# A selective-scan layer: a chunk's preparation laid over 19 states instead of 15, and the norm after the scan with its 1/std per token

## The chip, the cores and the metric

The kernel runs on one core of a Trainium2 chip. It computes a four-layer network in one launch; the change lies wholly in the first layer. The metric is the device time of one execution in microseconds (us). In the text PE is TensorE, DVE is VectorE, ACT is ScalarE, POOL is GpSimd and SP is SyncE, which only issues transfers here. Each engine runs its own instructions strictly in the order in which the program lists them, and waits where one of them needs something that another engine has not yet produced.

## The reference

Layer 0 is a two-dimensional selective scan over an image of 64 x 64 tokens, two images in the batch. After an input projection and a depthwise 3 x 3 convolution, the tokens are read in four orders (the four values of `kk`), and for each order a recurrence with 16 states per channel runs along the 4096 tokens of the image:

```python
delta = softplus(delta + delta_bias)
def step(h, inp):
    ut, dt, bt, ct = inp
    dA = exp(dt[..., None] * A4)
    h = dA * h + (dt * ut)[..., None] * bt[:, :, None, :]
    y = einsum('bkdn,bkn->bkd', h, ct)
    return (h, y)
...
y = y + u * D
# sum over the four orders, then
y = layernorm(y, eps=1e-5) * ln_w + ln_b     # over the 256 inner channels
y = y * silu(z)
x = x + y @ W_out.T
```

There are 256 inner channels (two halves of 128 partitions, `h` in the kernel), 16 states, and the result is added to the layer's input. Layers 1 to 3 (a deformable convolution, a state-space layer with a spectral filter, a linear attention and a mixture of experts) follow and are the same in both kernels.

## The kernel before, in words

`layer0` handles the two images one after the other. For each image it has three stages.

**Before the scan** (lines 195 to 236) it normalises, projects and convolves; the branch `z` goes to DRAM as `zs`, and the scan's input `U` stays in SBUF.

**The scan** (lines 238 to 406) goes through 32 chunks of 512 tokens, in the order given by `todo`: eight chunks for each of the four reading orders 0, 2, 1, 3. Inside a chunk there is a loop over the 16 states, `n`. One state is this chain:

- POOL multiplies `du` by one row of B, giving `S` (L365, 128 x 1024), and, except in the first chunk of an order, adds the state carried over from the chunk before (L371, two columns).
- ACT computes `dA = exp(dt * A)` in two halves (L374). There are two `dA` tiles, so ACT can be at most two states ahead of DVE.
- DVE runs the recurrence as one scan instruction over 1024 columns (L376), then multiplies the result by a row of C, `pcn`, giving `M` (L390).
- ACT saves the last column for the next chunk (L378). In the program this save comes one state later, between the next `dA` and that state's share of the preparation.
- PE spreads the row of C over the partitions (L334) and adds `M` up in `yp` through an identity matrix (L405).

`S` has four buffers: the product of state n can be started when `M` of state n-4 is done. B's rows come in groups of four, `br`, through DRAM, by a broadcast transfer that SP issues at n = 2, 6, 10 and 14 (L329). At n = 0 the sums of the chunk before are added to `Y` (`add_up`: on ACT for order 0, L345; on DVE otherwise, L341 and L347), and PE opens the new sums (L387).

Inside this loop the order of instructions is exactly that of the program (`tc.manual_schedule()`); outside it a planner orders them. Between L390 and L334 of each state one step of the generator `prologue` is taken: the preparation of the *next* chunk. Its pieces are separated by `yield`, and `next(steps, None)` takes one piece per state from n = 0; at n = 14 whatever is left is drained. There are 13 pieces, so the last is reached at n = 12:

| n | piece of the preparation |
|---|---|
| 0, 1 | ACT copies `uc`, one half each |
| 2 | PE: projection into PSUM |
| 3 | ACT copies it to `xd` and rounds it to `cs` (bf16); SP writes `bc` to DRAM; PE: first half of `pd` |
| 4, 5 | ACT: absolute value and relu of each half; PE: second half of `pd`; at 5 POOL: remainder `r` (L292) |
| 6 | ACT: two roundings of `r` into `cs` (L296, L297), exponential (L298) |
| 7 | POOL: second remainder (L300); ACT: `u = e + 1` (L301) |
| 8 | POOL: `dt += e` (L303); ACT: rounding (L304), logarithm (L305), with a table load before it and one after it |
| 9 | ACT: `u - 1` (L307) |
| 10, 11, 12 | POOL: `e - u` (L309), `dt += e` (L311), `du = dt * uc` (L313); ACT: `ea` (L318) |

Most tiles of the preparation have two buffers, one for the chunk in use and one for the chunk in preparation.

**The norm and the output projection** (lines 408 to 437) work through the 4096 tokens in eight blocks of 512, with the channels on the partitions: PE takes the mean by a matrix of 1/256 (`pm`), DVE subtracts it (L420), ACT squares (L421), PE averages again (`pq`), `rsqrt` computes 1/std for 128 x 512 values that are equal on all partitions (L81 to L87), DVE applies weight and 1/std (L429), then bias and gate (L430), PE projects to 128 tokens x 128 channels (L434), and DVE adds the result to `X` (L436).

Of the kernel before, what the change touches and what calls it, by code (L numbers as in the profile page):

```python
# [16 lines left out]
F32 = mybir.dt.float32  # L17
I32 = mybir.dt.int32
BF16 = mybir.dt.bfloat16
AF = mybir.ActivationFunctionType  # L20
# [138 lines left out]
def layer0(k):  # L159
# [3 lines left out]
    with ExitStack() as es:  # L163
# [13 lines left out]
            nc.vector.tensor_copy(sel[a : a + 16], k.ident[a : a + 16, a : a + 16].unsqueeze(2).to_broadcast([16, 16, P]))  # L177
        w_out = cst.tile([P, 2, C], F32, name="w_out")
        nc.sync.dma_start(out=w_out, in_=ins["w_out0"].rearrange("(a p) c -> p a c", p=P))
        mean_w = cst.tile([P, P], F32, name="mean_w")  # L180
        nc.vector.memset(mean_w, 1.0 / 256)
        an = cst.tile([P, 8, 16], F32, name="an")
# [9 lines left out]
        for b in range(B):  # L192
# [48 lines left out]
            with ExitStack() as e2:  # L241
# [12 lines left out]
                def prologue(kk, c, got):  # L254


                    uc = ch.tile([P, 2, T], F32, name="uc")
                    for h in range(2):
                        if kk % 2:
                            src = U[:, h, :].rearrange("p (g i w j) -> p w g j i", g=4, i=16, w=4)[:, c // 2, 2 * (c % 2) : 2 * (c % 2) + 2]  # L260
                            for g in range(2):
                                nc.scalar.copy(uc[:, h, g * 256 : (g + 1) * 256].rearrange("p (j i) -> p j i", j=16), src[:, g])
                        else:
                            src = U[:, h, (c // 2) * 1024 : (c // 2 + 1) * 1024].rearrange("p (i w j) -> p w i j", i=16, w=4)
                            for g in range(2):
                                nc.scalar.copy(uc[:, h, g * 256 : (g + 1) * 256].rearrange("p (i j) -> p i j", i=16), src[:, 2 * (c % 2) + g])
                        yield
                    px = ps.tile([P, N], F32, name="pd", tag="ps")
                    for h in range(2):
                        nc.tensor.matmul(px, w_xp[:, h, kk, :], uc[:, h, :], start=h == 0, stop=h == 1)  # L270
                    yield
                    xd = ch.tile([P, T], F32, name="xd")
                    nc.scalar.copy(xd, px)
                    bc = bcp.tile([16, T], F32, name="bc")
                    nc.sync.dma_start(out=bc, in_=xd[112:128, :])

                    cs = ch.tile([80, T], BF16, name="cs")
                    nc.scalar.copy(cs, xd[:80])


                    dt = ch.tile([P, 2, T], F32, name="dt")
                    du = ch.tile([P, 2, T], F32, name="du")
                    e = sm.tile([P, 2, T], F32, name="e")
                    u = sm.tile([P, 2, T], F32, name="u")
                    for h in range(2):
                        bias = k.v("dt_b")[:, kk * 2 + h : kk * 2 + h + 1]
                        pd = ps.tile([P, N], F32, name="pd", tag="ps")
                        nc.tensor.matmul(pd, w_dt[96:104, kk, h * P : (h + 1) * P], xd[96:104, :], start=True, stop=True)
                        yield
                        if h == 1:  # L290
                            r = sm.tile([80, T], F32, name="r")
                            nc.gpsimd.tensor_tensor(r, xd[:80], cs, ALU.subtract)  # L292
                        nc.scalar.activation(e[:, h, :], pd, AF.Abs, bias=bias)
                        nc.scalar.activation(dt[:, h, :], pd, AF.Relu, bias=bias)
                    yield
                    nc.scalar.copy(cs[32:64], r[32:64])  # L296
                    nc.scalar.copy(cs[64:80], r[64:80])  # L297
                    nc.scalar.activation(e, e, AF.Exp, scale=-1.0)  # L298
                    yield
                    nc.gpsimd.tensor_tensor(r[64:80], r[64:80], cs[64:80], ALU.subtract)  # L300
                    nc.scalar.activation(u, e, AF.Identity, bias=1.0)  # L301
                    yield
                    nc.gpsimd.tensor_tensor(dt, dt, e, ALU.add)  # L303
                    nc.scalar.copy(cs[64:80], r[64:80])  # L304
                    nc.scalar.activation(e, u, AF.Ln)  # L305
                    yield
                    nc.scalar.activation(u, u, AF.Identity, bias=-1.0)  # L307
                    yield
                    nc.gpsimd.tensor_tensor(e, e, u, ALU.subtract)  # L309
                    yield  # L310
                    nc.gpsimd.tensor_tensor(dt, dt, e, ALU.add)  # L311
                    yield
                    nc.gpsimd.tensor_tensor(du, dt, uc, ALU.mult)  # L313

                    ea = ch.tile([P, 16, 2], F32, name="ea")
                    f = T - 1 if kk >= 2 else 0
                    for h in range(2):
                        nc.scalar.activation(ea[:, :, h], an[:, kk * 2 + h, :], AF.Exp, scale=dt[:, h, f : f + 1])  # L318
                    got.append((uc, bc, cs, dt, du, ea))
# [7 lines left out]
                def spread(bc, q):  # L327
                    br = wk.tile([P, 4, T], F32, name="br", bufs=2)
                    nc.sync.dma_start(out=br, in_=bc[4 * q : 4 * q + 4, :].partition_broadcast(P))  # L329
                    return br  # L330
# [17 lines left out]

                with tc.manual_schedule():
                    rows, pcn, last, save = spread(ready[0][1], 0), c_row(ready[0][2], 0), None, None  # L350
                    for it, (kk, ci) in enumerate(todo):
                        c = at(it)[1]
                        uc, bc, cs, dt, du, ea = ready.pop()
# [2 lines left out]
                        if ci == 0:  # L356
                            for t in dAs:
                                nc.vector.memset(t[:, :, f : f + 1], 0.0)
                        steps = prologue(*at(it + 1), ready) if it + 1 < len(todo) else iter(())
                        s_ = slice(None, None, -1) if kk >= 2 else slice(None)  # L360
                        for n in range(16):
                            if n % 4 == 0:
# [25 lines left out]
                                last = kk, c, yp  # L388
                            M = wk.tile([P, 2, T], F32, name="M")
                            nc.vector.tensor_tensor(M, S, pcn.unsqueeze(1).to_broadcast([P, 2, T]), ALU.mult)  # L390
                            next(steps, None)
                            if n == 14:
                                for _ in steps:
                                    pass
                            if n < 15:
                                pcn = c_row(cs, n + 1)
# [9 lines left out]
                    add_up(*last)  # L406

            with ExitStack() as e2:
                wk = e2.enter_context(tc.tile_pool(name=f"l0f{b}", bufs=2))
                ps = e2.enter_context(tc.tile_pool(name=f"l0fs{b}", bufs=6, space=PSUM))  # L410
                for q in range(8):
                    s = slice(q * N, (q + 1) * N)
                    zt = wk.tile([P, 2, N], F32, name="zt")
                    nc.sync.dma_start(out=zt, in_=zs[:, :, b * L + q * N : b * L + (q + 1) * N].rearrange("h p t -> p h t"))
                    pm = ps.tile([P, N], F32, name="pm", tag="ps")
                    for h in range(2):
                        nc.tensor.matmul(pm, mean_w, Y[:, h, s], start=h == 0, stop=h == 1)
                    sq = wk.tile([P, 2, N], F32, name="sq")
                    for h in range(2):
                        nc.vector.tensor_tensor(Y[:, h, s], Y[:, h, s], pm, ALU.subtract)  # L420
                        nc.scalar.activation(sq[:, h, :], Y[:, h, s], AF.Square)  # L421
                    pq = ps.tile([P, N], F32, name="pq", tag="ps")
                    for h in range(2):
                        nc.tensor.matmul(pq, mean_w, sq[:, h, :], start=h == 0, stop=h == 1)
                    rs = wk.tile([P, N], F32, name="rs")
                    rsqrt(nc, wk, rs, pq, 1e-5, [P, N], "yn")
                    for h in range(2):
                        o = Y[:, h, s]
                        nc.vector.scalar_tensor_tensor(o, o, k.v("ln_w")[:, h : h + 1], rs, ALU.mult, ALU.mult)  # L429
                        nc.vector.scalar_tensor_tensor(o, o, k.v("ln_b")[:, h : h + 1], zt[:, h, :], ALU.add, ALU.mult)  # L430
                    po = ps.tile([P, N], F32, name="po", tag="ps")
                    for j in range(4):
                        for h in range(2):
                            nc.tensor.matmul(po[:, j * P : (j + 1) * P], Y[:, h, q * N + j * P : q * N + (j + 1) * P], w_out[:, h, :], start=h == 0, stop=h == 1)  # L434
                    o = Xb[:, 4 * q : 4 * q + 4, :]
                    nc.vector.tensor_tensor(o, po.rearrange("p (a c) -> p a c", c=C), o, ALU.add)  # L436
            yb.close()


# [1096 lines left out]
```

## Time and profile before

| | us |
|---|---|
| runs | 15821.19, 15821.78, 15835.69; median 15821.78 |
| the profiled execution | 15825.24 |
| its span in the profile | 15823.2 |
| layer 0, scan of the first image | about 141 to 2104 |
| norm of the first image | 2104 to 2254.6 |
| layer 0, scan of the second image | about 2380 to 4343 |
| norm of the second image | 4343 to 4494 |

The span is the time from the first to the last instruction of the profiled execution; some 2 us lie around it. Layer 0 takes the first 28% of it. Where rows of the profile are shown, a group's row has the line, engine, operation and tile, the number of instructions, their busy time in us and the mean of one in ns, and then the idle time of that engine just before them with what ended it. A row of the timeline has the start in us, the duration in us, and in brackets the idle time before it and its releaser.

### The profile page before, as it was taken

How to read it: one execution, taken by the hardware profiler on the slowest of the kernel's cores; microseconds unless marked ns; L12 is line 12 of the kernel's file. 1: busy time of each engine (PE TensorE's matmuls, PEld its weight loads, DVE VectorE, ACT ScalarE, POOL GpSimd, SP SyncE). 2: the span in 40 equal slices, each digit the busy share in tenths (PEclk: the TensorE clock that was granted, in tenths of full speed). 3: DMA queues.
4: the chain of work that ended last, by engine and by line, in shares of the span. 5: the costliest groups of instructions: out<-in, count | busy, mean ns of one | idle time of the engine just before them, and what ended most of it. 6: DMA issues, size and time to landing. Idle time of an engine off the chain costs nothing.

```text
span 15823.2 us, 190331 instructions
## 1 busy us (share of the span) xinstructions
PE 11939.5 (75%) x69390; PEld 7104.0 (45%) x69390; DVE 13880.2 (88%) x12178; ACT 9839.5 (62%) x15907; POOL 13460.9 (85%) x5140
## 2 busy tenths in 40 slices
PE   6666666666667744567887879879788898898897
PEld 2222222222247721234554546546445555555565
DVE  7999978999954389999999999999999999999974
ACT  5656626666510057777777777777777777777752
POOL 6888828888738889999999999999999999999960
PEclk9999989999978866778998989989999999999998
DMA  2111111111146534455565556556666665665643
GB/s 79 70 70 70 70 44 67 70 70 70 64 143 185 161 133 148 168 172 187 196 193 179 187 179 198 197 185 202 193 190 198 190 204 196 191 203 195 191 163 129
DMA packets 1211433, 2373.40 MB, mean 150 GB/s; under 512 B 346744, under 2 KB 923896, under 8 KB 1044352
## 3 DMA queue, kind: packets, MB, share of 16 engines
q1 hardware_dynamic: 1163072, 2206.74, 42.3%
q0 software_dynamic: 46560, 153.18, 3.2%
q8 instruction: 548, 8.98, 0.2%
q14 instruction: 389, 3.19, 0.1%
q10 hardware_dynamic: 864, 1.32, 0.0%
HBM read 2018.49 MB, written 342.41 MB: 149 GB/s over the span
## 4 chain that ended last, share of the span: by engine, by line
POOL 35%; PE 12%; DVE 11%; DMA 3%; ACT 2%; issue 2%; SPq 0%; POOLq 0%; ACTq 0%; DVEq 0%
POOL S L1110 34%; DVE S L1166 10%; PE pef L994 6%; PE Z L1128 2%; DMA row<-drow 2%; PE acc L967 2%; PE pw L793 1%; POOL S L1116 1%; ACT ze L1134 1%; ACT dA L1164 1%; DMA w<-in_w_b_dram 0%; PE acc L1029 0%; ACT e L974 0%; DMA e<-mdr 0%; PE pt L95 0%
## 5 line engine op out<-in xcount | busy, mean ns | idle before, releaser
L1166 DVE TENSOR_TENSOR_SCAN S<-dA,S 128x512 f32<-128x512 f32 x8192 | 9225.0, 1201 | 385.8 <-ACT dA L1164 207.0
L1110 POOL TENSOR_TENSOR S<-row,g 128x4096 f32<-128x4096 f32 x1024 | 9101.7, 8894 | 266.0 <-DMA row<-drow 224.2
L1164 ACT ACTIVATE dA<-row,a_t 128x512 f32<-128x512 f32 x8192 | 5615.6, 692 | 2141.3 <-DVE S L1166 2108.3
L1128 PE MATMUL Z<-S,cv 128*32 128x256 f32 x32768 | 2506.0, 436 | 1481.7 <-ACT ze L1134 1215.6
L994 PE MATMUL pef<-hk,ur 128*128 128x256 f32 x14336 | 3510.4, 388 | 131.8 <-ACT e L974 120.5
L994 PEld LDWEIGHTS pef<-hk,ur 128*128 128x128 f32 x14336 | 2645.3, 191 | 1070.8 <-issue 562.8
L376 DVE TENSOR_TENSOR_SCAN S<-dA,S 128x1024 f32<-128x1024 f32 x1024 | 2339.1, 2284 | 242.4 <-ACT dA L374 96.1
L365 POOL TENSOR_TENSOR S<-du,br 128x1024 f32<-128x1024 f32 x1024 | 2408.6, 2355 | 137.8 <-DVE M L390 81.0
L1128 PEld LDWEIGHTS Z<-S,cv 128*32 128x32 f32 x32768 | 1002.5, 121 | 2691.5 <-issue 1291.9
L405 PE MATMUL yp<-M,ident 128*128 128x512 f32 x4096 | 2054.6, 626 | 2.9 <-DVE M L390 2.9
L405 PEld LDWEIGHTS yp<-M,ident 128*128 128x128 f32 x4096 | 817.6, 200 | 2092.5 <-issue 2054.1
L374 ACT ACTIVATE dA<-dt,an 128x511 f32<-128x511 f32 x2048 | 1406.9, 687 | 208.1 <-DVE S L376 131.0
L390 DVE TENSOR_TENSOR M<-S,pcn 128x1024 f32<-128x1024 f32 x1024 | 1250.4, 1221 | 106.9 <-DVE S L376 3.7
L334 PE MATMUL pcn<-cs,sel 80*128 80x512 bf16 x1024 | 406.2, 397 | 1188.4 <-DVE M L390 1177.8
L1134 ACT COPY ze<-Z 128x512 f32<-128x512 f32 x1024 | 1123.1, 1097 | 232.4 <-PE Z L1128 200.3
L967 PE MATMUL acc<-e,mw 128*128 128x512 f32 x1920 | 1043.1, 631 | 30.6 <-ACT e L974 29.9
L569 POOL DMA_INDIRECT G<-table,idx x576 | 805.5, 1399 | 203.1 <-issue 170.6
L994 PEld LDWEIGHTS pef<-hd,ur 128*128 128x128 f32 x4096 | 757.8, 194 | 491.1 <-issue 235.2
L994 PE MATMUL pef<-hd,ur 128*128 128x256 f32 (+1 forms) x4096 | 876.4, 340 | 101.5 <-ACT e L974 94.4
L378 ACT COPY stt<-S 128x2 f32<-128x2 f32 x896 | 168.9, 189 | 1082.1 <-DVE S L376 1079.0
L576 DVE TENSOR_TENSOR G<-G,wt 128x4608 f32<-128x4608 f32 x64 | 317.4, 4960 | 572.9 <-DMA G<-table,idx 499.6
L974 ACT COPY e<-pef 128x512 f32<-128x512 f32 x960 | 557.8, 587 | 109.9 <-PE pef L994 61.5
(327 smaller groups left out, 8052.3 us busy)
## 6 DMA issues: line engine op xcount, KB each, us to landing
row<-drow SPq DMA_DIRECT2D x1024, 1024.0 KB
br<-bc SPq DMA_DIRECT2D x256, 1024.0 KB
zd<-ze SPq DMA_DIRECT2D x1024, 256.0 KB
hk<-in_phi_dram SPq DMA_DIRECT2D x128, 576.5 KB
hk<-in_phi_dram SPq DMA_DIRECT2D x96, 704.5 KB
hd<-in_phi_dram SPq DMA_DIRECT2D x512, 128.5 KB
mw<-wdr SPq DMA_DIRECT2D x480, 128.0 KB
hk<-in_phi_dram SPq DMA_DIRECT2D x160, 320.5 KB
```

The costliest lines, as they stand in the source:

```text
L365: nc.gpsimd.tensor_tensor(S, du, br[:, n % 4, :].unsqueeze(1).to_broadcast([P, 2, T]), ALU.mult)
L374: nc.scalar.activation(dA[:, h, rest], dt[:, h, rest], AF.Exp, scale=an[:, kk * 2 + h, n : n + 1])
L376: nc.vector.tensor_tensor_scan(flat, dflat, flat, 0.0, ALU.mult, ALU.add)
L390: nc.vector.tensor_tensor(M, S, pcn.unsqueeze(1).to_broadcast([P, 2, T]), ALU.mult)
L405: nc.tensor.matmul(yp[:, h, :], k.ident, M[:, h, :], start=False, stop=n == 15)
L967: nc.tensor.matmul(acc.rearrange("p a s -> p (a s)"), ms[f][:, o, :], e, start=box["first"], stop="whole" in box and (f, o) == todo[-1])
L994: nc.tensor.matmul(pe[:, a, 256 - n :], ur[:, par, j, :], h[:, at : at + n], start=i == 0, stop=i + 1 == len(mm))
L1110: nc.gpsimd.tensor_tensor(S, row.unsqueeze(1).to_broadcast([P, 2, R, T]), g.unsqueeze(2).to_broadcast([P, 2, R, T]), ALU.mult)
L1128: nc.tensor.matmul(Z[32 * j : 32 * j + 32, q], cv[:, h, s], S[:, h, :, s], start=h == 0, stop=h == 1)
L1134: nc.scalar.copy(ze.rearrange("p q t e -> p q e t"), Z)
L1164: nc.scalar.activation(dA, row[:, j % R, :], AF.Exp, scale=a_t[:, h, d : d + 1])
L1166: nc.vector.tensor_tensor_scan(s, dA, s, 0.0, ALU.mult, ALU.add)
```

## The change

There are two separate parts.

In the scan, three `yield` are added to the preparation: one ahead of the first remainder on POOL (L292), one ahead of the second (L300), and one ahead of `e - u` (L309). That makes 16 pieces. The generator of a chunk is now created two chunks ahead, at n = 12, and waits in the list `soon`; each state takes one piece of every generator in the list. A chunk's preparation so has the states 12 to 15 of one chunk and 0 to 14 of the next, 19 in all, and its last piece is reached at n = 11; the drain at n = 14 stays. The preparation of the very second chunk of an image begins at n = 0, having no earlier chunk to begin in.

In the norm, `mean_w[:, 0:1]` becomes the moving operand and the squares the stationary one, so that the variance comes out with a token per partition: `pv[:, j]`, 128 x 4 values for a block. 1/std is computed on those. Weight and bias of the norm are folded once, at the start, into two copies of the output matrix, `w_ow` and `w_ob`. The gate `z` is applied to the centred `Y` without 1/std; PE then makes two projections, the gated one with `w_ow` and that of the gate with `w_ob`, and DVE multiplies the first by 1/std while it adds both to `X`. The blocks are written so that block q is centred ahead of the projection of block q-1, and the pool has three buffers instead of two.

```diff
+        w_ow = cst.tile([P, 2, C], F32, name="w_ow")
+        w_ob = cst.tile([P, 2, C], F32, name="w_ob")
+        for h in range(2):
+            nc.gpsimd.tensor_scalar(w_ow[:, h, :], w_out[:, h, :], k.v("ln_w")[:, h : h + 1], None, ALU.mult)
+            nc.gpsimd.tensor_scalar(w_ob[:, h, :], w_out[:, h, :], k.v("ln_b")[:, h : h + 1], None, ALU.mult)
...
                         if h == 1:
+                            yield
                             r = sm.tile([80, T], F32, name="r")
                             nc.gpsimd.tensor_tensor(r, xd[:80], cs, ALU.subtract)
...
                     nc.scalar.activation(e, e, AF.Exp, scale=-1.0)
                     yield
+                    yield
                     nc.gpsimd.tensor_tensor(r[64:80], r[64:80], cs[64:80], ALU.subtract)
...
                     nc.scalar.activation(u, u, AF.Identity, bias=-1.0)
+                    yield
                     yield
                     nc.gpsimd.tensor_tensor(e, e, u, ALU.subtract)
...
+                    soon = []
...
-                        steps = prologue(*at(it + 1), ready) if it + 1 < len(todo) else iter(())
+                        if it == 0:
+                            soon.append(prologue(*at(1), ready))
...
-                            next(steps, None)
-                            if n == 14:
-                                for _ in steps:
+                            if n == 12 and it + 2 < len(todo):
+                                soon.append(prologue(*at(it + 2), ready))
+                            for steps in soon:
+                                next(steps, None)
+                            if n == 14 and it + 1 < len(todo):
+                                for _ in soon.pop(0):
                                     pass
...
-                wk = e2.enter_context(tc.tile_pool(name=f"l0f{b}", bufs=2))
+                wk = e2.enter_context(tc.tile_pool(name=f"l0f{b}", bufs=3))
...
+                    nc.scalar.activation(sq, Y[:, :, s], AF.Square)
+                    nc.vector.tensor_tensor(Y[:, :, s], Y[:, :, s], zt, ALU.mult)
+                    return zt, sq
+
+                def projected(q, zt, sq):
+                    pv = ps.tile([P, N], F32, name="pv", tag="ps")
                     for j in range(4):
                         for h in range(2):
+                            nc.tensor.matmul(pv[:, j : j + 1], sq[:, h, j * P : (j + 1) * P], mean_w[:, 0:1], start=h == 0, stop=h == 1)
+                    rs = wk.tile([P, 4], F32, name="rs")
+                    rsqrt(nc, wk, rs, pv[:, :4], 1e-5, [P, 4], "yn")
+                    po = ps.tile([P, 4, C], F32, name="po", tag="ps")
+                    pb = ps.tile([P, 4, C], F32, name="pb", tag="ps")
+                    for o, src, w in ((pb, lambda h, j: zt[:, h, j * P : (j + 1) * P], w_ob), (po, lambda h, j: Y[:, h, q * N + j * P : q * N + (j + 1) * P], w_ow)):
+                        for j in range(4):
+                            for h in range(2):
+                                nc.tensor.matmul(o[:, j, :], src(h, j), w[:, h, :], start=h == 0, stop=h == 1)
                     o = Xb[:, 4 * q : 4 * q + 4, :]
+                    nc.vector.tensor_tensor(o, pb, o, ALU.add)
+                    for j in range(4):
+                        nc.vector.scalar_tensor_tensor(o[:, j, :], po[:, j, :], rs[:, j : j + 1], o[:, j, :], ALU.mult, ALU.add)
+
+                behind = None
+                for q in range(8):
+                    got = centred(q)
+                    if behind is not None:
+                        projected(q - 1, *behind)
+                    behind = got
+                projected(7, *behind)
```

What is left out of the diff in the norm is the old chain: the second average `pq`, `rsqrt` on 128 x 512, L429, L430 and the addition L436.

More of the change, by code (lines that the diff above doesn't have):

```diff
@@ L408, in layer0, with centred @@
             with ExitStack() as e2:
-                wk = e2.enter_context(tc.tile_pool(name=f"l0f{b}", bufs=2))
+                wk = e2.enter_context(tc.tile_pool(name=f"l0f{b}", bufs=3))
                 ps = e2.enter_context(tc.tile_pool(name=f"l0fs{b}", bufs=6, space=PSUM))
-                for q in range(8):
+                def centred(q):
                     s = slice(q * N, (q + 1) * N)
@@ L420, in layer0 @@
                         nc.vector.tensor_tensor(Y[:, h, s], Y[:, h, s], pm, ALU.subtract)
[L421 to L430, printed above, removed]
@@ L431, in layer0 @@
-                    po = ps.tile([P, N], F32, name="po", tag="ps")
+                    nc.scalar.activation(sq, Y[:, :, s], AF.Square)
[3 more added lines that the diff above has]
+                    pv = ps.tile([P, N], F32, name="pv", tag="ps")
                     for j in range(4):
                         for h in range(2):
-                            nc.tensor.matmul(po[:, j * P : (j + 1) * P], Y[:, h, q * N + j * P : q * N + (j + 1) * P], w_out[:, h, :], start=h == 0, stop=h == 1)
@@ L435, in layer0 @@
-                    o = Xb[:, 4 * q : 4 * q + 4, :]
-                    nc.vector.tensor_tensor(o, po.rearrange("p (a c) -> p a c", c=C), o, ALU.add)
+                            nc.tensor.matmul(pv[:, j : j + 1], sq[:, h, j * P : (j + 1) * P], mean_w[:, 0:1], start=h == 0, stop=h == 1)
[3 more added lines that the diff above has]
+                    pb = ps.tile([P, 4, C], F32, name="pb", tag="ps")
```

## The prediction

> **What bounds the kernel now.** I read busy time by stage first: the scan of image 0, then its norm. Columns: stretch, length, then PE, PEld, DVE, ACT and POOL busy, PE's granted clock, DMA share, GB/s.
>
> ```profile
> 141.00:2100.00 1959.00, 1313.40 (x2929) 521.40 (x2929) 1805.45 (x1076) 1186.34 (x2136) 1641.02 (x1203) 0.96 0.19 69
> 2104.00:2180.00 76.00, 31.60 (x97) 18.90 (x97) 44.36 (x51) 8.63 (x13) 0.00 (x0) 0.73 0.09 28
> ```
>
> The scan is DVE's (92%); POOL is close behind (84%). In the norm nobody is busy: DVE has 58%, so a chain across engines is the limit. Next the waits of layer 0, for DVE's scan and for POOL:
>
> ```profile
> POOL r L292 <- ACT cs L278: 364.5, 64, 105.3
> POOL r L300 <- ACT cs L297: 182.5, 64, 3.4
> DVE S L376 <- ACT dA L374: 96.1, 74, 2.4
> DVE S L376 <- POOL S L371: 84.6, 104, 1.8
> POOL e L309 <- ACT u L307: 78.6, 58, 2.8
> DVE S L376 <- POOL S L365: 57.3, 10, 25.5
> ```
>
> DVE loses 242 us ahead of its scans; 51 of the last row are the two images' first states. The timeline of one chunk (state 0 at 692.77, a state every 3.525) shows where the rest sits:
>
> ```profile
> 714.30 1.15 POOL L300 TENSOR_TENSOR r<-r,cs 16x512 f32<-16x512 f32 x1 [2.86 <-ACT cs L297]
> ...
> 725.78 2.29 DVE L376 TENSOR_TENSOR_SCAN S<-dA,S 128x1024 f32<-128x1024 f32 x1 [1.20 <-ACT dA L374]
> ...
> 726.82 2.35 POOL L309 TENSOR_TENSOR e<-e,u 128x1024 f32<-128x1024 f32 x1 [1.19 <-ACT u L307]
> ...
> 736.68 2.29 DVE L376 TENSOR_TENSOR_SCAN S<-dA,S 128x1024 f32<-128x1024 f32 x1 [0.24 <-POOL S L371]
> ...
> 741.57 2.29 DVE L376 TENSOR_TENSOR_SCAN S<-dA,S 128x1024 f32<-128x1024 f32 x1 [1.26 <-POOL S L371]
> ```
>
> These are n = 9, 12 and 13, alike in nearly every chunk: 1.20 at n = 9 (sum 67), 0.24 at n = 12 (12), 1.27 at n = 13 (74). At n = 1 another 27, most of it 1.8 to 2.4 in the chunks behind order 0, where ACT copies `Y`. Now one norm block:
>
> ```profile
> 2123.71 1.28 DVE L420 TENSOR_TENSOR Y<-Y,pm 128x512 f32<-128x512 f32 x2 [0.17 <-PE pm L417]
> ...
> 2128.53 3.35 DVE L83 RECIPROCAL rs<-yn_s 128x512 f32<-128x512 f32 x1 [0.69 <-ACT yn_s L82]
> ...
> 2136.68 0.50 PEld L434 LDWEIGHTS po<-w_out,Y 128*128 128x128 f32 x2 [10.41 <-DVE Y L430]
> ...
> 2142.21 0.69 DVE L436 TENSOR_TENSOR X<-po,X 128x512 f32<-128x512 f32 x1 [4.92 <-PE po L434]
> ```
>
> The next block's L420 is at 2143.25: no overlap, 18.8 per block, 150.9 for eight (2103.7 to 2254.6).
>
> **What the Trainium skill says.** "TensorE: Matmul & The Clock Gate", section "What's actually happening", has PE at half clock after an idle window of about 3.4 us and at full clock after a busy one. The trace agrees in direction: 0.96 in the scan, 0.73 in the norm, in steps of 0.5 and 1.0. "GPSIMD Engine Reference", section 4.1, puts two-input elementwise work on POOL at about twice DVE's time; here 2355 ns (L365) against 1221 (L390, same shape). "ScalarE: Activation LUTs", section "What ACT_TABLE_LOAD costs", states 1283 ns and a drain of 1380; this trace has 1283 and the logarithm 0.02 us after it, so I price the load alone.
>
> **The scan, part by part.** No instruction is added. Set state 0's scan to 0 and take state n's at 3.525n. POOL may start product n when `M` of n-4 ends, at 3.525n - 10.6; product, two-column add and gaps take 2.6 (product starts lie 2.58 to 2.6 apart); so POOL can be 8.0 ahead and regains 0.92 per state. Each extra 2.35 costs 2.3, `r` 1.1.
>
> *Before.* `r` at n = 5 stalls 2.4 for ACT. L300 needs L297, done at 21.4 (n = 6), and starts at 21.5. Then product 8 at 22.7, L303, products 9 and 10, `e - u` at 34.0 after 1.2 of waiting, and product 13 is ready at 48.9 against 47.5 due (with the 1.2 of n = 9). That is the measured 1.27: the chain reproduces it.
>
> *After.* Positions: `r` n = 2, L296 to L298 n = 3, L300 n = 5, L303 and the logarithm n = 6, L307 n = 7, L309 n = 9, L311 n = 10, `du` n = 11. `cs` is rounded at n = 15 of the chunk before, ends at -1.9, so `r` at -0.1 finds it. L297 ends at 10.8; POOL comes at 9.6 and waits 1.2, to 12.0. Product 6 then L303: 17.0; product 7: 19.6; 8: 22.2; 9: 24.8. L307 ends at 27.0 (logarithm and both loads at 20.1 to 24.4, `dA`): wait 2.2; L309 29.4; product 10 32.0; L311 34.3; product 11 36.9; `du` 39.3; product 12 ready at 41.9, due 43.4. DVE is not stopped. **Gone: 12 + 74, and about 4 of n = 9's that were POOL's.**
>
> *What stays.* Logarithm and two loads (0.61 + 1.28 + 1.06 + 1.28) move from n = 8 to n = 6; ACT's room between save and next `dA` is about 3.1. The 1.2 reappears at n = 7, 60 times.
>
> *What is late next.* At n = 0 ACT now has `abs` and `relu` (1.37) where it copied half of `uc` (0.81): behind the `Y` copies of order 0 that is 0.57 x 16 = **+9**. On PE the second `pd` (0.9) now stands at n = 0 between L387 and the row of C for n = 1. In orders 1 and 3 that row ends at 7.04 and `M` reads it at 8.15; 7.9 still fits. At half clock it doesn't: three of the first 24 chunks have it, so **+4** with the second chunk's denser preparation. At n = 15 ACT's `xd` waits for PE's projection (two 512-column products behind four of `yp`); by the same sequence at n = 3 before, the following `dA` ends 0.5 before its scan. The rounding of `cs` also waits there for the last reader of the tile two chunks back, L334 at n = 14, already past. SP's queue: `bc` now stands at n = 15, ahead of the broadcast of n = 2, which is issued at -2.0 instead of about -5 and lands 5 later (711.2 to 716.5 in the trace), at 3.0; POOL wants it at 3.5 or later. Scan: -90 + 13 = **-77**, bounds -35 (half the lateness stays at n = 10 to 12) and -95.
>
> **The norm.** Work of one block after. PE: `pm` 4 x 0.43; `po` and `pb` 32 x 0.112 (pitch in the fast part of 2159.6 to 2160.5); `pv` 16 x 0.108 (pitch of L136's pair, one column): 7.0. At half clock 4 x 0.85 + 32 x 0.213 + 16 x 0.17 = 12.9. DVE: L420 1.37; gating 1.22 (as L390); 1/std on 128 x 4 1.36 (the six at 2266.68 to 2268.05 in the group norm); bias sum 0.69; four multiply-adds 0.25 each, from L429's 0.75 for 512 columns: 5.6. ACT 1.3. Gone from DVE: 3.35, 4 x 0.69, 0.43, 2.8. Since block q+1 is centred first, PE never waits for DVE and is the bound. A PE without pauses should mostly hold full clock; I take 8.6 a block, plus 4 to fill and 1.5 to drain: 74 against 151, **-76 per image, -152**. Bounds: 7.0 gives 62 (-178 in all), 12.9 gives 109 (-84). The four folding instructions on POOL (0.6 each, as L217) lie in the first 118 us, where POOL is busy 10. What follows the norm starts when its memory comes free, so it moves up one to one.
>
> **Sum.** -77 - 152 = -229. The profiled execution's 15825.2 becomes 15596; it lies 3.5 above the median shown, so from the median: **15593**. No change is taken as within 0.2% (32 us).
>
> **Rivals.**
> - *POOL's lateness only moves* to n = 10 to 12: for it, three 2.35 in a row and 1.5 of slack at n = 12; against it, the same chain gave n = 13 before to 0.1. Scan +13, sum -139: 15683.
> - *PE stays at half clock in the norm* (0.73 now): norm -84, sum -161: 15661.
> - *Slower: the chunk boundary.* If PE runs at half clock around n = 14 to 1, `yp` and the projection take 3.4 each, `xd` is ready at 7.6 after `M` of 13, `dA` at 10.3 instead of 7.05: 3.3 x 62. The opening sums, `pd` and row at n = 1 end 2.5 late in 48 chunks. 205 + 120 - 90 + 9 - 152: +92, 15914. It decides from about 4 us per boundary. For it: half-clock stretches at 746 to 753. Against: they follow the stall at n = 13, which goes.
> - *The planner* puts the blocks in sequence again and POOL's lateness moves: at half clock a serial block is about 18.5, so near 15820.
>
> **Chances.** Forecast 0.74 (own range 15555 to 15650), POOL 0.10, half clock 0.09, boundary 0.04, planner 0.03. Range 15555 to 15690, reaching to the first two rivals. Faster 0.93, same 0.03, slower 0.04.
>
> **What would show it.** Right: no idle ahead of the scans at n = 12 and 13, 1.2 at n = 7 left, POOL's wait at L292 gone but for the start, L300's near 1.2; a norm near 75 with PE as its busiest engine and a clock near 0.9. Wrong: DVE waiting for `dA` at n = 0 or for `pcn` at n = 1, POOL for `br`, or a norm over 110.

## The result, and the profile after

The changed kernel runs in 15606.35 us (median of four runs, 15597.23 to 15611.47) against 15828.74 for the kernel before (median of four, with the runs taken on the same chip). The ratio is 0.9859, with a 95% interval of 0.9842 to 0.9876: 222 us less at the medians. The forecast was 15593, or 229 less. The profiled execution took 15611.47, its span is 15609.7.

So the gain was forecast to 7 us. Its two terms were not: the scan gave less than forecast and the norm more. The stage table shows it; the columns are stretch, length, busy PE, PEld, DVE, ACT, POOL, then PE's granted clock, DMA share and GB/s. The first row is the scan of image 0, the second its norm.

```profile
143.00:2076.00 1933.00, 1286.47 (x2933) 510.35 (x2932) 1801.42 (x1078) 1185.40 (x2133) 1639.51 (x1201) 0.97 0.19 70
2076.00:2136.10 60.10, 57.98 (x415) 50.20 (x414) 39.85 (x113) 10.83 (x17) 0.00 (x0) 0.97 0.15 45
```

| us, from the timelines | before | after | change | forecast |
|---|---|---|---|---|
| scan, image 0 and image 1 | 1960.2, 1959.8 | 1933.0, 1935.5 | -51.5 | -77 |
| norm, image 0 and image 1 | 150.9, 151.0 | 60.1, 60.3 | -181.5 | -152 |
| between norm 0 and scan 1 | 128.3 | 127.5 | -0.8 | none |

In the norm PE has 58 of 60 us and its clock is 0.97: it has become the bound, as forecast. In the scan DVE is busy as long as before, and what it waits for has changed. The waits of layer 0, with total, number and longest:

```profile
POOL r L299 <- ACT cs L284: 188.6, 2, 101.4
...
POOL e L318 <- ACT u L315: 138.6, 64, 3.3
...
DVE S L387 <- ACT dA L385: 101.9, 75, 2.3
...
POOL r L308 <- ACT cs L304: 65.1, 58, 1.9
...
DVE M L401 <- PE pcn L343: 51.9, 34, 3.2
...
DVE S L387 <- POOL S L376: 51.7, 2, 26.3
```

POOL's wait for the first rounding is left only in the two preparations ahead of the loop (count 2 instead of 64); for the second it is 65.1 / 58 = 1.1 each (forecast 1.2), for `u` 138.6 / 64 = 2.2 (forecast 2.2). DVE's scan no longer waits for POOL at all, but for the first state of each image: the 86 us at n = 12 and 13 are gone. State by state in the timeline, 63.7 of the 101.9 waiting for `dA` lies at n = 7, 1.19 in each of 54 chunks, where the logarithm's step has moved.

The row that was not expected at this size is the fifth. DVE's second operation, `M`, waits for the row of C, and 50.9 of the 51.9 lies at n = 1 of the chunks in orders 1 and 3. One such chunk (the scan of its state 0 starts at 1643.15), in the timeline:

```profile
1645.42 2.41 DVE L350 TENSOR_TENSOR Y<-yp,Y 128x512 f32<-128x512 f32 x2
...
1647.98 3.54 PE L398 MATMUL yp<-uc,dd 128*128 128x512 f32 x4 [2.60 <-DVE Y L350]
...
1651.45 1.19 PE L294 MATMUL pd<-xd,w_dt 8*128 8x512 f32 x2
1652.57 0.39 PE L343 MATMUL pcn<-cs,sel 80*128 80x512 bf16 x1
...
1653.00 1.22 DVE L401 TENSOR_TENSOR M<-S,pcn 128x1024 f32<-128x1024 f32 x1 [1.84 <-PE pcn L343]
```

While DVE adds the old sums to `Y`, PE pauses 2.60. Then the four products that open the new sums take 3.54, `pd` stands behind them, and the row of C ends 9.8 after the scan of state 0; `M` would have started at 8.15. The same place in the kernel before has the same pause, but the products at full speed:

```profile
1675.62 1.95 PE L387 MATMUL yp<-uc,dd 128*128 128x512 f32 x4 [2.61 <-DVE Y L341]
1677.41 0.38 PE L334 MATMUL pcn<-cs,sel 80*128 80x512 bf16 x1
```

The clock's record says why: in the changed kernel it is at half from 5.1 to 8.5 after the scan of state 0. In the kernel before, the half-clock stretch of most chunks of these orders sat near -7 to -3.5, behind a pause of PE at the stall of n = 13 (2.79 in one of them). Of the 32 openings of the sums in orders 1 and 3, both images taken together, 7 were slowed in the kernel before (over 2.3 us instead of 1.96), and 29 are slowed now.

Some of the gain is not seen at the end of the span: the two traces are 234 apart when layer 0 ends and 214 at the end. The 20 drift back over the 11350 us of layers 1 to 3, which are the same in both; in the traces of the ten experiments below it is between -2 and 28. The runs of one kernel are 14 to 17 apart, and the cause of the drift stays open.

### The profile page after: what moved, and what is told of

It reads as the page before. It is cut to its first block, busy times and chain, and to the rows that moved or that the text cites. A ratio compares the mean times of both kernels' runs of the same rounds, so it can differ in the third digit from the quotient of the medians.

```text
span 15609.7 us, 191436 instructions
## 1 busy us (share of the span) xinstructions
PE 11894.2 (76%) x69838; PEld 7117.6 (46%) x69838; DVE 13768.3 (88%) x12194; ACT 9829.7 (63%) x15891; POOL 13474.0 (86%) x5144
## 4 chain that ended last, share of the span: by engine, by line
POOL 35%; PE 14%; DVE 11%; DMA 3%; ACT 2%; issue 2%; SPq 0%; POOLq 0%; ACTq 0%; DVEq 0%
POOL S L1139 34%; DVE S L1195 10%; PE pef L1023 7%; PE Z L1157 2%; PE acc L996 2%; DMA row<-drow 2%; PE pw L822 1%; POOL S L1145 1%; ACT dA L1193 1%; ACT ze L1163 1%; DMA w<-in_w_b_dram 0%; PE acc L1058 0%; DMA e<-mdr 0%; ACT e L1003 0%; DMA w<-in_w_c_dram 0%
## 5 line engine op out<-in xcount | busy, mean ns | idle before, releaser
L1023 PE MATMUL pef<-hk,ur 128*128 128x256 f32 x14336 | 3507.0, 388 | 137.8 <-ACT e L1003 122.0
L387 DVE TENSOR_TENSOR_SCAN S<-dA,S 128x1024 f32<-128x1024 f32 x1024 | 2338.0, 2283 | 161.2 <-ACT dA L385 101.9
L419 PE MATMUL yp<-M,ident 128*128 128x512 f32 x4096 | 1974.5, 604 | 2.9 <-DVE M L401 2.9
L401 DVE TENSOR_TENSOR M<-S,pcn 128x1024 f32<-128x1024 f32 x1024 | 1250.4, 1221 | 151.9 <-PE pcn L343 51.9
L613 ACT COPY vt<-pv 128x512 f32<-128x512 f32 (+1 forms) x192 | 88.4, 480 | 864.9 <-remote 598.0
```

The lines of the kernel that those rows point to most:

```text
L387: nc.vector.tensor_tensor_scan(flat, dflat, flat, 0.0, ALU.mult, ALU.add)
L419: nc.tensor.matmul(yp[:, h, :], k.ident, M[:, h, :], start=False, stop=n == 15)
L1023: nc.tensor.matmul(pe[:, a, 256 - n :], ur[:, par, j, :], h[:, at : at + n], start=i == 0, stop=i + 1 == len(mm))
```

## The experiments

The theory, A: POOL met ScalarE's results too early, stalled in its own order, and what it lost there reached DVE at n = 12 and 13; the three extra steps remove that. The earlier start isn't needed for it, and costs something at the chunk's boundary. Its rival, B: the earlier start, 19 states instead of 15, is what makes room. Of the norm it was open how much comes from the order of the blocks and how much from the smaller work.

**Each part alone.** The changed scan with the old norm:

```diff
-            (the new norm, w_ow, w_ob)
+            (the norm of the kernel before)
```

> The changed scan with the old norm. If the two parts act apart: scan of an image 1933 to 1936 (1960 before), norm still 151, layer 0 ends near 4390 instead of 4494, the whole about 103 shorter than before. DVE waits for the row of C at n = 1 some 50 in all, nothing at n = 12 and 13, 64 at n = 7. Rival, that the scan's gain in the changed kernel came partly from the new norm (memory or planner): scan longer than 1945.

Ratio 0.9971 (0.9959 to 0.9983), scans of 1932.0 and 1939.0, norm 150.8; layer 0 ends 47.8 earlier than before. The "103" and "4390" in the expectation were a slip of mine: twice 26 is 52, not 103. The lengths of the scan lie within 3 of what is written, and the 52.1 us of waiting for the row of C are as written. The rival, a scan longer than 1945, falls.

And the changed norm behind the old scan:

> The old scan with the changed norm. If the parts act apart: norm 60 per image instead of 151 with TensorE at full clock and 7.1 a block, scan 1960 as before, the whole about 181 shorter than before. Rival, that the norm was only fast because of what the scan left behind (clock, memory): norm 75 or more.

Ratio 0.9886 (0.9871 to 0.9901), 181 less at the medians. The old scan is 1958.7 long, the first image's norm 58.4 with PE at full clock (the second's is 61.9):

```profile
2102.60:2161.00 58.40, 56.29 (x415) 48.57 (x414) 39.83 (x112) 10.83 (x17) 0.00 (x0) 1.00 0.16 46
```

46 + 181 = 227 against 222 for both: the parts add.

**The three extra steps alone**, from n = 0 as before, with the old norm:

```diff
                         if h == 1:
+                            yield
                             r = sm.tile([80, T], F32, name="r")
...
                     nc.scalar.activation(e, e, AF.Exp, scale=-1.0)
                     yield
+                    yield
...
                     nc.scalar.activation(u, u, AF.Identity, bias=-1.0)
+                    yield
                     yield
```

> The three extra steps alone: the preparation starts at n = 0 as before, has 16 pieces, the last two together at n = 14; old norm. Theory A, the steps do the work (GpSimd stalled for ScalarE, and that lateness reached DVE): worked by the same chain, product 15 is ready at 53.3 against 54.0 due, so no wait at n = 12 to 15; scan 1918 per image, shorter than the changed kernel's 1934, because the second half of pd does not stand at n = 0; the whole about 85 shorter than before. Rival B, the earlier start does the work: three GpSimd operations at n = 13 and 14 make products 15 and 0 late by 1 to 2, scan about 1960 as before.

Ratio 0.9941 (0.9928 to 0.9955), 92 less; scans of 1911.8 and 1913.5, which is 22 per image *shorter* than in the changed kernel. DVE's waits in layer 0:

```profile
DVE S L379 <- ACT dA L377: 96.7, 76, 1.8
...
DVE S L379 <- POOL S L368: 52.7, 3, 25.5
...
DVE M L393 <- PE pcn L337: 8.7, 17, 0.7
```

POOL stops DVE only at the images' first states, but for one wait of 1.8. This decides for A, and says more: the earlier start costs 43 us of what the steps bring. Which of the three steps are needed wasn't run.

The row of C, without `pd` ahead of it, costs 8.7 instead of 52, although the half clock is here too: it slows 21 of the 32 openings. In the chunk whose state 0 starts at 1328.09:

```profile
1332.96 3.51 PE L390 MATMUL yp<-uc,dd 128*128 128x512 f32 x4 [2.62 <-DVE Y L344]
1336.30 0.38 PE L337 MATMUL pcn<-cs,sel 80*128 80x512 bf16 x1
...
1336.72 1.22 DVE L393 TENSOR_TENSOR M<-S,pcn 128x1024 f32<-128x1024 f32 x1 [0.58 <-PE pcn L337]
```

The opening is as slow as in the changed kernel, but the row follows it at once and ends 8.6 after the scan of state 0, not 9.8.

**The earlier start alone**, with the old 13 pieces:

```diff
-                            yield          (the three extra ones)
```

> The earlier start alone: the preparation begins at n = 12 of the chunk before, has the old 13 pieces, the last at n = 8; old norm. Theory A: GpSimd stalls at n = 1, 3 and 6 as it did at 5, 7 and 10, and products 8 and 9 come 0.4 and 1.4 late; with the wait at n = 1 for the row of C the scan is 1960 to 1985, so no gain. Rival B: scan near 1934 as in the changed kernel.

Ratio 1.0077 (1.0064 to 1.0091): slower, by 118. Scans of 2018.9 and 2023.4.

```profile
DVE S L379 <- ACT dA L377: 163.4, 131, 2.4
DVE S L379 <- POOL S L374: 79.8, 102, 1.3
...
DVE M L393 <- PE pcn L335: 56.4, 32, 3.2
```

B falls. POOL's lateness is back, and lies at n = 8 and 9 (12 and 73 in all; 0.2 and 1.2 a chunk, where 0.4 and 1.4 were expected). That each scan is 34 to 38 longer than the top of the expected range was not foreseen. In the timeline, 48 over both images, 24 of each, is a wait for `dA` at n = 2, 0.9 to 1.1 in each of 44 chunks: without the extra step the second `abs` and `relu` are due at n = 1, but their `pd` comes only behind the products that open the sums, and ACT holds the next `dA` back. In an order-1 chunk at half clock `pd` ends at 9.5 and `dA` at 12.1, where 11.1 was due; in an order-2 chunk at full clock they end at 6.7 and 9.3, where 8.2 was due. So this wait is the place of `pd`, at either clock.

**What is behind the wait for the row of C?** In the changed kernel, copies of one product keep PE busy in the pause:

```diff
+                            if n == 15 and kk % 2 and ready:
+                                for _ in range(8):
+                                    nc.tensor.matmul(pcn, sel[:, 0, :], ready[0][2], start=True, stop=True)
```

> The changed kernel with eight more copies of the product L343 behind the last sums of a chunk in orders 1 and 3: TensorE does no useful work with them, but has no pause while VectorE adds the sums up. Theory C, the wait for the row of C at n = 1 is TensorE's half clock, set by that pause: the row ends near 8.0 after the scan of state 0 instead of 9.7, the wait falls from 52 to under 15 in all, scan of an image 1914 instead of 1934. Rival D, it is the second half of pd standing there at whatever clock: the wait stays near 50.

One run, 15575.31. Scans of 1915.9 twice. PE in the same chunk, whose state 0 starts at 1636.37:

```profile
1638.44 1.89 PE L422 MATMUL pcn<-cs,sel 80*128 80x512 bf16 x8
1641.23 1.96 PE L398 MATMUL yp<-uc,dd 128*128 128x512 f32 x4 [0.90 <-DVE Y L350]
1643.12 1.12 PE L294 MATMUL pd<-xd,w_dt 8*128 8x512 f32 x2
1644.17 0.39 PE L343 MATMUL pcn<-cs,sel 80*128 80x512 bf16 x1
```

With eight useless products the pause is 0.90, the opening products take 1.96 instead of 3.54, and the row ends 8.2 after the scan of state 0. The wait falls from 52 to 15. Rival D, the place of `pd` at whatever clock, falls; but C alone is not the whole either. With the row due at 8.15, the traces have all four cases: neither, the row ends at 7.04 (before); the half clock alone, about 8.5, a wait of mostly 0.3 to 0.7 (the steps alone); `pd` alone, 8.2, a listed wait of 0.19; both, about 9.7, a wait of mostly 1.7 (the changed kernel). Each of the two nearly fits into the 1.1 of room, and only together they cost DVE much.

The other way round, the products are taken out of that place:

```diff
-                                for h in range(2):
-                                    nc.tensor.matmul(yp[:, h, :], dd[:, kk * 2 + h, :], uc[:, h, :], start=True, stop=False)
...
+                            if n == 2:
+                                for h in range(2):
+                                    nc.tensor.matmul(yp[:, h, :], dd[:, kk * 2 + h, :], uc[:, h, :], start=False, stop=False)
...
-                                nc.tensor.matmul(yp[:, h, :], k.ident, M[:, h, :], start=False, stop=n == 15)
+                                nc.tensor.matmul(yp[:, h, :], k.ident, M[:, h, :], start=n == 0, stop=n == 15)
```

> The changed kernel with the D term (L398) added at n = 2 instead of opening the sums at n = 0. If what queues ahead of the row of C on TensorE is the cause (C or D alike), the wait at n = 1 goes: 52 to under 5, scan 1934 to near 1910. If DVE waits for something else in that place, another wait of 1.7 comes up in orders 1 and 3.

One run, 15562.72, scans of 1914.2 and 1913.4. The wait at n = 1 is gone; 6.7 in all come up at n = 3, behind the moved products. Taking the products out of the queue ahead of the row serves as well as filling the pause.

**Toward a better version.** The steps without the earlier start, with the new norm:

> The three extra steps without the earlier start, and the changed norm. The measured parts add: scan 1912, norm 59 to 60, the whole 92 + 181 = 273 shorter than the kernel before, near 15560, about 45 below the changed kernel. If the earlier start has a use together with the new norm: not below the changed kernel.

15567.81 (15562.00 to 15577.81), ratio 0.9831 (0.9817 to 0.9844), 269 less than before where 273 were expected; scans of 1913.8 and 1910.8, norm 61.8. Then ScalarE's rounding L304 moved out of the logarithm's step:

```diff
-                    nc.scalar.copy(cs[64:80], r[64:80])
                     nc.scalar.activation(e, u, AF.Ln)
                     yield
+                    nc.scalar.copy(cs[64:80], r[64:80])
                     nc.scalar.activation(u, u, AF.Identity, bias=-1.0)
```

> As the run before, with ScalarE's rounding L304 taken one step later, out of the step with the logarithm and its two table loads. The wait of 1.2 for dA behind that step is the sum of its four parts against ScalarE's room: without 0.61 of it the wait is 0.58, 35 less over 60 chunks, the whole near 15525. If the wait is only the table loads' and not the sum: it stays near 67 in all.

15523.39 (15522.09 to 15528.43), ratio 0.9802 (0.9789 to 0.9816): 314 less than before, the best of all, and below the changed kernel (0.9842 to 0.9876) clear of both intervals. Scans of 1896.7 and 1894.0.

```profile
DVE S L384 <- ACT dA L382: 57.5, 73, 1.8
```

It was 102.8 in the run before. At n = 11 the wait fell from 67.3 to 31.4: the step's length against ScalarE's room, as written.

**What made the norm short?** First the new norm with its blocks in sequence:

```diff
-                behind = None
-                for q in range(8):
-                    got = centred(q)
-                    if behind is not None:
-                        projected(q - 1, *behind)
-                    behind = got
-                projected(7, *behind)
+                for q in range(8):
+                    projected(q, *centred(q))
```

> The changed kernel with the norm's blocks written one after the other, centred and projected, instead of block q+1 centred ahead of block q's projection. If the overlap makes a good part of the norm's 91: a block is then a chain of mean 1.9, subtraction 1.3, square 1.1, variance 1.8, two projections 3.8 and the four additions 1.1, about 11.5 with the waits, and a norm is 85 to 110 instead of 60. If the planner overlaps the blocks by itself, or TensorE is the bound in either order: 60 to 65.

Norm 100.8 (one run, 15694.22), PE busy 79 of it at a clock of 0.78:

```profile
2080.50:2181.30 100.80, 79.33 (x415) 69.15 (x414) 41.82 (x112) 11.37 (x17) 0.00 (x0) 0.78 0.09 27
```

The instructions are the same as in the overlapped norm; PE's busy time is 21 longer, since it pauses and its clock drops. Then the old instructions in the new order:

```diff
+                def centred(q):       (zt, mean, L420, L421)
+                def projected(q, zt, sq):   (pq, rsqrt on 128 x 512, L429, L430, L434, L436)
+                (the loop with `behind`)
```

> The changed kernel with the old norm's instructions (1/std on 128 x 512 values, weight and bias on VectorE) in the new order: block q+1 centred ahead of block q's rest, three buffers. If the order alone brought most of the gain: 60 to 90. If VectorE's work matters too: its 11.4 per block, with the waits for the root and for the projection, give 14 to 16, a norm of 110 to 130.

137.8 (one run, 15779.82), 8 above the range:

```profile
2077.80:2215.60 137.80, 59.25 (x191) 37.14 (x190) 90.13 (x105) 16.05 (x25) 0.55 (x1) 0.71 0.09 30
```

DVE has 90 of 138. In its timeline there is still a wait of 4.38 for the projection at the end of a block: the new order gives it nothing to do there, as the next centring stands behind the addition to `X`. So 151 becomes 138 by the order, 101 by the work, 60 by both: the order is worth 13 with the old work and 41 with the new. The third buffer is in both of these runs; what it brings by itself wasn't run.

## Why the prediction was right

**POOL's lateness: right, and its cause shown.** The chain gave -90 for n = 12, 13 and part of 9. The waits at n = 12 and 13 are all gone. The two forecast stalls of POOL (1.2 and 2.2) came out at 1.1 and 2.2, and the chain's other use, the three steps from n = 0, was confirmed to about 6 us of scan length (1918 expected, 1912 and 1913.5 measured). The rival "POOL's lateness only moves" is what happened in the run with the early start alone, not in this change.

**What stays: right.** The wait behind the logarithm reappeared at n = 7, 63.7 in all.

**What is late next: mis-sized.** Two terms stood there. Behind the order-0 copies +9 was forecast; n = 1 rose from 27 to 33.5, +6. The other, "+4" for the row of C at half clock in "three of the first 24 chunks", is the step that failed: it measured 51 at n = 1. What one such chunk costs was seen rightly, a row that no longer fits; how many there would be was not, 29 of 32 openings in orders 1 and 3 (even the trace of before has 7, over both images). I had taken the place of the half-clock stretches from the trace of before. Most of them stood behind the stall at n = 13 that the change removes, and I counted that removal as safety in the rival of the chunk's boundary ("they follow the stall at n = 13, which goes"). In fact the stretch then fell behind the next pause, at the opening of the sums, mostly 1.7 to 2.5 at a time. A wait for `pcn` at n = 1 was one of the signs named for "wrong", and it came. The rival's second half came true in most chunks of orders 1 and 3, at less than its 2.5; its first half, `dA` late at n = 0, did not: `dA` ends 0.52 ahead of the scan, where 0.5 was forecast. The Trainium skill, "TensorE: Matmul & The Clock Gate", section "What's actually happening", asks for an idle window of about 3.4 us; here a pause of 2.60 was enough, with a half-clock stretch of 3.4 behind it. The last section shows from the traces when it is.

The sum of the scan is not closed by these rows. The waits ahead of DVE's scans and for the row of C fall by 31 in all (192.8 to 161.3, the images' first states left out), the two scans by 51.5. A scan that has not waited starts 0.08 before the recorded end of the product ahead of it, so each of the 111 waits ahead of scans that went took about 0.08 more than is listed, 9 in all; the rest, about 10, I have not placed.

**The norm: right mechanism, rate too careful.** 7.0 per block at full clock was worked out from rows of before; 8.6 was taken, for a clock not always full. Measured, `pm` to `pm`:

```profile
2101.11 1.88 PE L433 MATMUL pm<-Y,mean_w 128*128 128x512 f32 x4
2102.83 1.84 PE L445 MATMUL pv<-mean_w,sq 128*128 128x1 f32 x16
2104.53 2.03 PE L453 MATMUL pb<-w_ob,zt 128*128 128x128 f32 x16
2106.40 1.95 PE L453 MATMUL po<-w_ow,Y 128*128 128x128 f32 x16
2108.19 1.88 PE L433 MATMUL pm<-Y,mean_w 128*128 128x512 f32 x4
```

7.08 a block, without a pause. The gain of 181.5 lies at the favourable bound that the forecast gave (178). The two misses, 26 and 29 us, are of opposite sign and nearly cancel: that the total came within 7 is luck.

**The rest.** SP's new order cost nothing to be seen: none of POOL's waits in the scan is ended by a transfer of `br`. The stage between norm and second scan is 0.8 shorter, so the norm's gain was passed on whole.

## What to carry to other kernels

When a producer engine stalls in its own order, look at where its inputs are made and put a step between them before giving the work a longer run-up: here three empty steps brought the whole gain of the scan, and the earlier start took a good part of it back. A moved piece is to be checked on every queue it joins, at the slow clock too, above all where that queue has just paused and somebody waits for its next result. And in a chain that no engine fills, shorter work and an overlapping order are worth more together than the sum of each alone (here 13 and 50, and 91 together).

## What the runs showed of the hardware

TensorE's half clock moves: with one pause removed, the same slow stretch of 3.4 us fell behind a pause of 2.60 in another place, where before, behind a pause of 2.61, it had mostly not been. Eight useless products that cut the pause to 0.90 restored 1.96 us for what had taken 3.54.

When a pause is followed by the slow stretch can be worked out from the traces. In each of them all changes in the clock's record lie on a fixed grid of 3.413 us, to within 0.015. I cut the two scans, from the second chunk on, along this grid and took PE's busy share in every piece at full clock. Before, 82 such pieces are followed by one at half clock, and PE was busy at most 0.41 of each; 930 are followed by full clock, and PE was busy at least 0.42 of each. In the changed kernel it is 50 pieces with at most 0.41 and 976 with at least 0.43. So the pause needn't be as long as a piece, but enough of it must lie within one. In the chunk of before shown above, the grid cuts the pause: the piece from 1671.36 to 1674.77 has PE busy for 0.48 of it, and full clock follows. In the changed kernel's chunk, the piece from 1644.79 to 1648.20 holds the whole pause, with PE busy for 0.24, and half clock follows. Nine of the ten other traces divide at the same share, one of them (the eight useless products) with a single exception. The tenth is the run that opens the sums late: 22 of its 79 pieces ahead of a slow stretch have PE busy for more. All 22 hold `pd`, whose products use 8 of the 128 rows, and if `pd` is counted as idle they fit too. So busy time is not quite the measure.

It also fits that the slow stretch came nearly every time. In the changed kernel most of the slowed chunks last 61.4 to 61.7, which is 18.0 to 18.1 pieces of the grid, so the pause of the next chunk meets the grid at the same place; most of the chunks with the eight useless products last 59.99, or 17.6 pieces. No run shifted the grid alone, so this last step is argued.

In the norm at full clock, 16 instructions of 128 columns in fp32, each with its load of weights, take 1.95 to 2.03, about 0.11 from one to the next. Sixteen of one column take 1.84: the time hardly follows the columns there.
